# Splitting the mode mixing and the first GroupNorm into two halves of eight images

## The chip, the cores and the metric

The kernel runs on one core of one Trainium2 chip. The metric is the device time of one execution in microseconds (us), the median of three runs. Of one further execution there is a profile, taken by the hardware profiler.

## The reference

The input x has 16 images of 64 channels and 128 x 128 pixels, all in float32. Two layers are computed.

Layer 0: `x_ht = dht_2d(x)` (a Hartley transform); the lowest 20 x 20 modes are mixed over the channels, `0.5 * (e(x1, w1) - e(x1n, w1n) + e(x1, w1n) + e(x1n, w1))` with `e = einsum('bixy,ioxy->boxy')` and `n` for the mirrored mode; the result is transformed back, smoothed by a Gaussian along **all four** axes (images and channels too), and masked.

Layer 1, on that result: `h = group_norm(x)` in eight groups of channels; `afno(h)` (a Fourier transform, 32 x 32 modes, two complex block-diagonal layers with a Gelu between, the inverse transform) plus `h` plus `x`; a second group norm; `feats = gelu(conv1x1(h))`; two shared experts; a gating network on the mean of `feats` that picks 4 of 16 experts for each image; the sum of all of them plus the residual.

## The kernel before

The program is one long list of statements. A scheduler turns it into one queue for each engine and places every wait; a queue runs strictly in order.

**Forward (L239 to L266).** For each image b of 16, eight tiles `xt` (128 x 8 x 128, 512 KB) are loaded by SP (L245) into a pool of 10 buffers. TensorE multiplies each by `fwd1` (L250), ScalarE copies the product into `t1` (L253). After the second tile of the next image, `along_columns` takes the second axis: TensorE (L212), a ScalarE copy (L215), six VectorE additions (L219 to L222), and one VectorE operation for each of up to nine neighbouring images, which adds the Gaussian over images into `x2` (L231, L233). Image `bo` of `x2` is therefore final only when image `bo + 4` has passed. ScalarE then writes its mirrored second copy (L236, L237). Eleven pairs of loads bring the weights `wk` and `wn`.

**Mixing (L283 to L321).** For each of 11 values of k1, 20 matmuls with 64 weight columns and 64 moving columns (16 images, two copies, two modes; L294) fill one PSUM tile `psm`, which ScalarE and VectorE take turns to copy into `om` (L298 to L303). Then 128 small matmuls blur over channels (L312), and copies (L319, L321) make `ot`, 100 modes on the partitions.

**GroupNorm 1 (L397 to L471).** From `ot`: means (L397), deviations by a triangular matrix `dev` (L406), squared by ScalarE (L408), summed by `ones` (L412). The two halves of the images stand on the two halves of the partitions. A chain of small VectorE operations gives the scales `gs1`, and `st` for the modes.

**Fourier products (L539 to L565).** For each image and each half n of 1,024 modes: eight matmuls by the matrix `spec` (L548), VectorE scaling into `xk` (L552, L554), and, one step behind, the first complex layer (L499) with its Gelu (L501), stored to DRAM `o1d` (L503). `modes` (L480, L483) runs once for each of the first ten images, `modes_out` (L488 to L491) for the next four; it writes `od` and `ond` to DRAM, which the next stage reads back into `bm` (L611).

**Image stage (L571 to the end).** All the rest of layer 1, image by image, by a written-out order.

A matmul in float32 is recorded as two MATMUL and two LDWEIGHTS records, so a count of records is twice the count of matmuls. The profile numbers lines by this kernel:

Of the kernel before, what the change touches and what calls it, by code (L numbers as in the profile page):

```python
# [159 lines left out]
def hartley_afno_moe_kernel(ctx: ExitStack, tc: tile.TileContext, a: dict, out: bass.AP):  # L160
# [14 lines left out]
    on_modes = ExitStack()  # L175
    otp = on_modes.enter_context(tc.tile_pool(name="ot", bufs=1, side="right"))
    ot = otp.tile([CH, 4, NB * C], F32, name="ot")
# [9 lines left out]
    with tc.tile_pool(name="modes", bufs=1) as mp:  # L187

        x2 = mp.tile([P, 2, NB, NM], F32, name="x2")
        wk = mp.tile([P, K // 2 + 1, K, C], F32, name="wk")
        gb = blur_matrix(NB)
        with tc.tile_pool(name="f_x", bufs=10) as xp, tc.tile_pool(name="f_t", bufs=2) as tp, \
                tc.tile_pool(name="f_c", bufs=1) as fc, \
                tc.tile_pool(name="f_p1", bufs=4, space=PSUM) as pp1, \
                tc.tile_pool(name="f_p2", bufs=2, space=PSUM) as pp2:
            fwd1 = load(fc, "fwd1", [P, W1], nc.gpsimd)
            fwd2 = None

            wn = fc.tile([P, K, C], F32, name="wn")
            seen = set()

            def along_columns(b, t1):


                ps = pp2.tile([P, K // 2, W1], F32, name="ps2")
                for m in range(K // 2):
                    for t in range(2):
                        for h in range(2):  # L210
                            j = 2 * (2 * m + h) + t
                            nc.tensor.matmul(ps[h * C:(h + 1) * C, m, :], lhsT=t1[:, j, :],  # L212
                                             rhs=fwd2[:, j, :], start=(t == 0), stop=(t == 1))
                pn = tp.tile([P, K // 2, K], F32, name="pn")
                nc.scalar.copy(pn, ps[:, :, K:2 * K])  # L215
                xm = tp.tile([P, K, K], F32, name="xm")
                for half, op in ((0, ALU.add), (1, ALU.subtract)):
                    to = xm[half * C:(half + 1) * C]
                    nc.vector.tensor_tensor(to[:, 0:1], ps[0:C, 0:1, 0:K], pn[0:C, 0:1], op)  # L219
                    nc.vector.tensor_tensor(to[:, 2:K:2], ps[0:C, 1:, 0:K],  # L220
                                            pn[0:C, K // 2 - 1:0:-1], op)
                    nc.vector.tensor_tensor(to[:, 1:K:2], ps[C:P, :, 0:K],  # L222
                                            pn[C:P, ::-1], op)
                xf = xm.rearrange("p a b -> p (a b)")
                for bo in range(NB):
                    g = float(gb[bo, b])
                    if g == 0.0:
                        continue
                    to = x2[:, 0, bo, :]
                    if bo in seen:  # L230
                        nc.vector.scalar_tensor_tensor(to, xf, g, to, ALU.mult, ALU.add)  # L231
                    else:
                        nc.vector.tensor_scalar(to, xf, g, None, ALU.mult)  # L233
                        seen.add(bo)
                    if not gb[bo, b + 1:].any():
                        nc.scalar.mul(x2[0:C, 1, bo], x2[C:P, 0, bo], -1.0)  # L236
                        nc.scalar.copy(x2[C:P, 1, bo], x2[0:C, 0, bo])  # L237

            behind = None  # L239
            for b in range(NB):  # L240

                t1 = tp.tile([P, 2 * K, C], F32, name="t1")
                for c0 in range(0, C, 8):
                    xt = xp.tile([P, 8, N], F32, name="xt")
                    nc.sync.dma_start(xt, a["x"][b, :, c0:c0 + 8])  # L245
                    ps = pp1.tile([P, 8, W1], F32, name="ps1")
                    for i in range(8):
                        for h in range(2):
                            cols = slice(h * 64, (h + 1) * 64)
                            nc.tensor.matmul(ps[cols, i, :], lhsT=xt[:, i, cols],  # L250
                                             rhs=fwd1, start=True, stop=True)
                    src = ps[:, :, 0:2 * K].rearrange("p c j -> p j c")
                    nc.scalar.copy(t1[:, :, c0:c0 + 8], src)  # L253
                    if c0 == 8 and behind:
                        along_columns(*behind)
                behind = (b, t1)
                fwd2 = fwd2 or load(fc, "fwd2", [P, 2 * K, W1])

                if 0 < b <= K // 2 + 1:
                    k = b - 1  # L260
                    nc.scalar.copy(wk[C:P, k, 0], wn[C:P, 0])
                    nc.scalar.copy(wk[C:P, k, 1:K], wn[C:P, K - 1:0:-1])
                if b <= K // 2:
                    nc.sync.dma_start(wk[0:C, b], a["w"][b])
                    nc.sync.dma_start(wn[C:P], a["w"][(-b) % K])
            along_columns(*behind)  # L266

        sc = on_modes.enter_context(tc.tile_pool(name="s_c", bufs=1, side="right"))
        blurc = load(sc, "blurc", [P, C])
        dev = load(sc, "dev", [CH, 4, NM])  # L270
        mean = load(sc, "mean", [CH, 4, C])
        gn1 = load(sc, "gn1", [P, 2, C])
        ident = load(sc, "ident", [P, C])
        sel = load(sc, "sel", [CH, 5, 32])
        w1 = load(sc, "w1", [P, 2, P])
        vec = load(const, "vec", [P, V_N])
        spec = load(sc, "spec", [CH, 4, 2 * MD * MD])
        exw = load(sc, "exw", [P, C, NE])

        with tc.tile_pool(name="m_o", bufs=1) as op, \  # L280
                tc.tile_pool(name="m_p", bufs=2, space=PSUM) as pp, \
                tc.tile_pool(name="m_p2", bufs=4, space=PSUM) as pp2:


            om = [op.tile([P, NB, NM // 2], F32, name=f"om{h}") for h in range(2)]
            lok, upk = (t[h * C:(h + 1) * C].rearrange("o b (k2 k1) -> o k1 k2 b", k1=K)
                        for h, t in enumerate(om))
            for k1 in range(K // 2 + 1):

                ps = pp.tile([P, K // 2, 2, NB, 2], F32, name="psm")  # L290
                for m in range(K // 2):
                    k = k1 * K + 2 * m
                    for h in range(2):
                        nc.tensor.matmul(ps[h * C:(h + 1) * C, m].rearrange("p a b q -> p (a b q)"),  # L294
                                         lhsT=wk[:, k1, 2 * m + h, :], rhs=x2[:, :, :, k:k + 2],
                                         start=True, stop=True)
                lo, up = ps[0:C, :, :, :, 0], ps[C:P, :, :, :, 1]
                nc.scalar.copy(lok[:, k1], lo[:, :, 0])  # L298
                nc.vector.tensor_copy(upk[:, k1], up[:, :, 0])
                if k1 % (K // 2):  # L300
                    nc.scalar.copy(lok[:, K - k1, 0:1], lo[:, 0:1, 1])
                    nc.scalar.copy(lok[:, K - k1, K // 2 - 1:0:-1], lo[:, 1:, 1])
                    nc.vector.tensor_copy(upk[:, K - k1, ::-1], up[:, :, 1])  # L303


            for b0 in range(0, NB, 8):
                for cc in range(2):
                    pq = [pp2.tile([CH, 8, C], F32, name="pst") for h in range(2)]
                    for i in range(8):
                        for h, (m0, m1) in ((0, (0, C)), (1, (C, CH)), (1, (0, C)), (0, (C, CH))):  # L310
                            g = slice(h * C, (h + 1) * C)
                            nc.tensor.matmul(pq[h][m0:m1, i, :],  # L312
                                             lhsT=om[h][g, b0 + i, cc * CH + m0:cc * CH + m1],
                                             rhs=blurc[g], start=True, stop=True)
                    for h in range(2):
                        dst = ot[:, 2 * h + cc, b0 * C:(b0 + 8) * C]
                        src = pq[h].rearrange("p b c -> p (b c)")
                        if h:
                            nc.scalar.copy(dst, src)  # L319
                        else:  # L320
                            nc.vector.tensor_copy(dst, src)  # L321
# [49 lines left out]
    with tc.tile_pool(name="s_w", bufs=2) as sw, tc.tile_pool(name="s_o", bufs=1) as so, \  # L371
# [38 lines left out]
        for rc in range(4):  # L410
            for (g, cols), sq in zip(halves, sqs):
                nc.tensor.matmul(psv[g], lhsT=ones[:CH], rhs=sq[:, rc], start=(rc == 0), stop=(rc == 3))  # L412
# [547 lines left out]
```

## Time and profile before

| | |
|---|---|
| Three runs | 1852.95, 1852.01, 1849.28 us; median 1852.01 |
| Profiled execution | 1848.89 us, span 1846.9 us, mean granted clock 0.976 |
| TensorE, VectorE, ScalarE, GpSimd busy | 92 %, 69 %, 75 %, 7 % of the span |

By stage, from the view of busy time by windows of core 0 (us from the span's start):

| Stage | Window | Length | TensorE busy | Granted clock | DMA share |
|---|---|---|---|---|---|
| last part of the forward | 207.0 to 253.4 | 46.4 | 36.83 | 0.96 | 0.63 |
| TensorE waits for `x2` | 253.4 to 261.4 | 8.0 | 0 | 0.71 | 0.19 |
| channel products (L294) | 261.4 to 289.3 | 27.9 | 20.52 | 0.74 | 0.60 |
| blur over channels (L312) | 289.3 to 296.4 | 7.1 | 6.44 | 0.64 | 0.25 |
| GroupNorm 1 (L397, L406, L412) | 296.4 to 320.9 | 24.5 | 24.50 | 1.00 | 0.11 |
| Fourier products | 320.9 to 472.5 | 151.6 | 150.19 | 1.00 | 0.26 |
| image stage | 472.5 to 1846.9 | 1374.4 | 1314.43 | 0.99 | 0.26 |

How to read it: busy is the time in which at least one record of the engine ran; a DMA share of 1 means that all 16 DMA engines of the core were busy; the granted clock is what the throttle let TensorE have, 1 being full speed.

### The profile page before, as it was taken

What the parts mean: (1) busy time and instruction counts of PE and PEld (TensorE: products, weight loads), DVE (VectorE), ACT (ScalarE), POOL (GpSimd) and SP (SyncE); (2) the same over time, 40 slices, a digit from 0 to 9 for tenths busy, and PEclk for the clock granted to TensorE, in tenths of its full rate; (3) what the DMA queues carried; (4) which work ended last, traced back from release to release, by engine and by line L of the source; (5) the groups of instructions that cost most, each with busy time, mean ns of one, the idle gap of its engine ahead of it and who ended that gap; (6) DMA issues with size and microseconds to landing.
All of it is one profiled execution on the core that took longest, in us unless ns stands there. A gap on an engine that the chain in (4) does not pass through costs nothing. (4 is left out here: it accounts for less than half of the span.)

```text
span 1846.9 us, 55817 instructions
## 1 busy us (share of the span) xinstructions
PE 1701.5 (92%) x24644; PEld 940.8 (51%) x24644; DVE 1270.7 (69%) x1774; ACT 1378.3 (75%) x1690; POOL 120.9 (7%) x140
## 2 busy tenths in 40 slices
PE   6777769999899999999999999999999999999996
PEld 6776765333645455454545555454545455554521
DVE  1233432322249788797979797797979797887988
ACT  2343343112488998989898999989898999989897
POOL 0000002003010101010110101010100101010110
PEclk8899988999999999999999999999999999999998
DMA  9999841115212222222332222322232322222023
GB/s 337 319 322 326 285 145 48 69 52 145 47 25 70 48 81 57 84 36 82 57 72 58 59 82 36 99 41 81 37 86 53 71 72 46 72 57 71 27 72 92
DMA packets 136129, 181.00 MB, mean 98 GB/s; under 512 B 94201, under 2 KB 95414, under 8 KB 135658
## 3 DMA queue, kind: packets, MB, share of 16 engines
q1 hardware_dynamic: 132192, 171.73, 33.1%
q0 software_dynamic: 3696, 5.71, 1.2%
q8 instruction: 193, 3.16, 0.7%
q14 instruction: 48, 0.39, 0.1%
HBM read 98.29 MB, written 79.11 MB: 96 GB/s over the span
## 5 line engine op out<-in xcount | busy, mean ns | idle before, releaser
L834 DVE SCALAR_TENSOR_TENSOR h<-g,wt,h 128x1024 f32<-128x1024 f32 x512 | 620.9, 1275 | 85.2 <-ACT g L831 85.2
L831 ACT ACTIVATE g<-pe,wl 128x1024 f32<-128x1024 f32 x512 | 539.4, 1131 | 8.9 <-PE pe L826 8.2
L826 PE MATMUL pe<-f,wl 64*64 64x512 f32 x4096 | 494.7, 600 | 1.3 <-issue 0.4
L834 DVE SCALAR_TENSOR_TENSOR h<-g,h 128x1024 f32<-128x1024 f32 x256 | 301.6, 1220 | 56.1 <-ACT g L831 56.1
L831 ACT ACTIVATE g<-pe,vec_sb 128x1024 f32<-128x1024 f32 x256 | 278.7, 1135 | 20.6 <-PE pe L826 20.4
L669 PEld LDWEIGHTS pe<-inv_sb,u 107*128 107x128 f32 x2048 | 234.4, 192 | 64.9 <-ACT g L831 33.2
L826 PEld LDWEIGHTS pe<-f,wl 64*64 64x64 f32 x4096 | 135.6, 132 | 237.3 <-ACT g L831 98.6
L826 PE MATMUL pe<-f,shw 64*64 64x512 f32 x2048 | 252.9, 604 | 0.0
L669 PE MATMUL pe<-inv_sb,u 107*128 107x128 f32 x2048 | 248.8, 279 | 3.2 <-ACT g L831 1.9
L677 ACT ACTIVATE h<-pe,gs 128x1024 f32<-128x1024 f32 x128 | 142.6, 1115 | 73.2 <-PE pe L669 57.3
L250 PE MATMUL ps<-fwd_sb,xt 128*64 128x64 f32 x4096 | 141.5, 232 | 51.0 <-issue 43.1
L681 DVE BATCH_NORM_STATS2 stats<-h 128x6 f32<-128x512 f32 x256 | 160.1, 679 | 25.9 <-ACT h L677 25.8
L250 PEld LDWEIGHTS ps<-fwd_sb,xt 128*64 128x64 f32 x4096 | 135.9, 147 | 54.7 <-issue 46.6
L647 PE MATMUL pe<-inv_sb,bm 64*64 64x128 f32 (+1 forms) x4096 | 144.8, 275 | 1.2 <-issue 1.2
L736 ACT ACTIVATE f<-pe,fb 128x1024 f32<-128x1024 f32 x128 | 144.3, 1137 | 2.2 <-PE pe L732 2.2
L647 PEld LDWEIGHTS pe<-inv_sb,bm 64*64 64x64 f32 (+1 forms) x4096 | 118.5, 124 | 48.1 <-ACT f L736 24.3
L253 ACT COPY t<-ps 128x320 f32<-128x320 f32 x128 | 54.0, 427 | 114.4 <-PE ps L250 114.0
L732 PE MATMUL pe<-h,fs 64*64 64x512 f32 x1024 | 133.9, 611 | 1.6 <-DVE n L709 1.6
L652 ACT COPY u<-pe 105x1024 f32<-105x1024 f32 x128 | 127.4, 1043 | 3.9 <-PE pe L647 2.9
L219 DVE TENSOR_TENSOR xm<-ps,pn 64x20 f32<-64x20 f32 x32 | 5.5, 171 | 172.5 <-ACT pn L215 172.2
L548 PE MATMUL psx<-spec_sb,ot 100*64 100x512 f32 x512 | 115.6, 594 | 0.0
L806 POOL DMA_INDIRECT wl<-exd,ati x64 | 66.9, 1045 | 697.4 <-ACT g L831 605.4
(164 smaller groups left out, 1163.5 us busy)
## 6 DMA issues: line engine op xcount, KB each, us to landing
xt<-in_x_dram SPq DMA_DIRECT2D x128, 512.0 KB
out_dram<-h SPq DMA_DIRECT2D x256, 256.0 KB
o1d<-o SPq DMA_DIRECT2D x16, 512.0 KB
s<-o1d SPq DMA_DIRECT2D x16, 512.0 KB
bm<-od SPq DMA_DIRECT2D x96, 50.0 KB
wk<-in_w_dram SPq DMA_DIRECT2D x11, 320.0 KB
wn<-in_w_dram SPq DMA_DIRECT2D x11, 320.0 KB
spec_sb<-in_spec_dram SPq DMA_DIRECT2D x1, 3200.0 KB
```

What stands on the lines that cost most here:

```text
L250: nc.tensor.matmul(ps[cols, i, :], lhsT=xt[:, i, cols], rhs=fwd1, start=True, stop=True)
L548: nc.tensor.matmul(ps[ri * C:(ri + 1) * C], lhsT=ot[:, kc, b * C:(b + 1) * C], rhs=spec[:, kc, ri * 1024 + n * 512:ri * 1024 + (n + 1) * 512],
L647: nc.tensor.matmul(ps[cs, h, i, :], lhsT=bm[rs, 4 * q + i, cs], rhs=inv1[rs, part], start=True, stop=True)
L652: nc.scalar.copy(dst.rearrange("p h s n -> p n h s"), ps[0:KC].rearrange("p h s n -> p n h s"))
L669: nc.tensor.matmul(ps[:, r // 4, r % 4 * N:(r % 4 + 1) * N], lhsT=u[0:KU, 2 * row:2 * row + 2, :].rearrange("p h c -> p (h c)"), rhs=inv2, ...
L677: nc.scalar.activation(h, ps, AF.Identity, bias=gs1[:, 1, box["b"]:box["b"] + 1])
L681: nc.vector.bn_stats(box["stats"][:, 2 * t + p, :], h[:, p])
L732: nc.tensor.matmul(ps[p * C:(p + 1) * C, half], lhsT=box["fs"][rows_], rhs=box["h"][t][rows_, p], start=True, stop=True)
L736: nc.scalar.activation(f, ps, AF.Gelu, bias=box["fb"], accum_out=box["sums"][:, t:t + 1])
L826: nc.tensor.matmul(ps[half * C:(half + 1) * C, p], lhsT=w[rows_], rhs=f[rows_, half], start=True, stop=True)
L831: nc.scalar.activation(g, ps, AF.Gelu, bias=bias)
L834: nc.vector.scalar_tensor_tensor(h, g, share(), h, ALU.mult, ALU.add)
```

## The change

Mixing and GroupNorm 1 become a generator `behind_modes(h, ...)` that works on eight images (h = 0 or 1) and is advanced step by step among other work. Its first half is advanced once for each tile of the forward from image 12 on, when images 0 to 7 are final; its second half is advanced twice after each half of an image in the Fourier products of images 1 to 6. `x2` becomes `x3` with three blocks: the sums of images 0 to 7, one block of mirrored copies that both halves use in turn, and the sums of images 8 to 15. The constants are loaded after image 10's tiles and not after the forward; `spec` is loaded as eight tiles into the buffers of `xt`. Pools shrink: `xt` from 10 to 8 buffers, the forward's PSUM from 4 and 2 tiles to 3 and 1. `modes` and `modes_out` run after each half of images 8 to 14. The rest, the image stage included, is unchanged.

```diff
+    sc, sqp, xp = right("s_c", 1), right("s_q", 2), right("f_x", 8)
+    pm = on_modes.enter_context(tc.tile_pool(name="m_p", bufs=2, space=PSUM))
+    x3 = mp.tile([P, 3, HB, NM], F32, name="x3")
+    wn = om[1].rearrange("p b m -> p (b m)")[:, 0:K * C].rearrange("p (k c) -> p k c", c=C)
+    def second(bo):
+        sums = x3[:, bo // HB * 2, bo % HB]
+        nc.scalar.mul(x3[0:C, 1, bo % HB], sums[C:P], -1.0)
+        nc.vector.tensor_copy(x3[C:P, 1, bo % HB], sums[0:C])
...
+    def behind_modes(h, blurc, dev, mean, gn1, ident, sel, w1, vec):
+        if h:
+            for bo in range(HB, NB):
+                second(bo)
+                if bo % 2:
+                    yield
...
+        for k1 in range(K // 2 + 1):
+            ps = pm.tile([P, K // 2, 2, HB, 2], F32, name="psm")
+            for m in range(K // 2):
+                k = k1 * K + 2 * m
+                for i in range(2):
+                    nc.tensor.matmul(ps[i * C:(i + 1) * C, m].rearrange("p a b q -> p (a b q)"),
+                                     lhsT=wk[:, k1, 2 * m + i, :], rhs=x3[:, h:h + 2, :, k:k + 2],
+                                     start=True, stop=True)
...
+            yield
+        for cc in range(2):
+            pq = [pm.tile([CH, HB, C], F32, name="psm") for i in range(2)]
...
+            yield
...
+        psm = pm.tile([P, 512], F32, name="psm")
+        for kc in range(4):
+            nc.tensor.matmul(psm[g], lhsT=mean[:, kc, :], rhs=ot[h][:, kc], start=(kc == 0), stop=(kc == 3))
+        yield
...
+        for rc in range(5):
+            if rc < 4:
+                ps = pm.tile([P, 512], F32, name="psm")
+                for kc in range(rc, 4):
+                    nc.tensor.matmul(ps[:CH], lhsT=dev[:, kc, rc * CH:(rc + 1) * CH],
+                                     rhs=ot[h][:, kc], start=(kc == rc), stop=(kc == 3))
+                sq = sqp.tile([CH, 512], F32, name="sq")
+                nc.scalar.activation(sq, ps[:CH], AF.Square)
+                sqs.append(sq)
+            if rc:
+                nc.tensor.matmul(psv[g], lhsT=made["ones"][:CH], rhs=sqs[rc - 1], start=(rc == 1), stop=(rc == 4))
+            yield
...
+                if c0 == 8 and behind:
+                    along_columns(*behind)
+                if b == HB + 4 and c0 == 24:
+                    first = behind_modes(0, **consts)
+                elif first:
+                    next(first, None)
...
+            if b == K // 2:
+                consts = constants()
+        for n in range(2):
+            for kc in range(4):
+                t = xp.tile([P, 8, N], F32, name="xt")
+                spec[n, kc] = t[0:CH].rearrange("p a b -> p (a b)").rearrange("p (r j) -> p r j", r=2)
+                nc.sync.dma_start(spec[n, kc], src[:, kc, :, n])
+        along_columns(*behind)
+        for _ in first:
+            pass
...
+    last = behind_modes(1, **consts)
+    for b in range(HB - 1):
+        def between(n):
+            for _ in range(2 if b else 0):
+                next(last, None)
+        fourier(b, between)
+    for _ in last:
+        pass
+    mixing.close()
...
+        steps = [lambda m=m: modes(m) for m in range(K // 2)] + [lambda i=i: modes_out(i) for i in range(QB)]
+        for b in range(HB - 1, NB):
             if b == HB:
                 bn1s, bn1f, bn2s, bn2f = prepare()
+            def between(n):
+                if b >= HB and steps:
+                    steps.pop(0)()
+            fourier(b, between)
```

`fourier(b, between)` holds the Fourier products of one image as before and calls `between(n)` after each half. `consts` are the tiles that `constants()` loads.

## The prediction

> **What bounds the kernel now.** The chain of waits reaches back over the last few per cent only, so I read busy time by windows, cut where TensorE changes its work:
>
> ```profile
> core 0: us, PE busy (x) PEld busy (x) DVE busy (x) ACT busy (x) POOL busy (x), PEclk, DMA share, GB/s
> 207.00:253.40 46.40, 36.83 (x1153) 35.74 (x1149) 17.88 (x45) 15.95 (x39) 0.00 (x0) 0.96 0.63 221
> 253.40:261.40 8.00, 0.00 (x0) 0.00 (x0) 4.21 (x12) 5.59 (x11) 0.20 (x1) 0.71 0.19 55
> 261.40:289.30 27.90, 20.52 (x440) 19.42 (x440) 9.10 (x22) 9.84 (x35) 0.00 (x0) 0.74 0.60 161
> 289.30:296.40 7.10, 6.44 (x258) 6.24 (x258) 3.04 (x10) 4.37 (x16) 7.03 (x3) 0.64 0.25 67
> 296.40:320.90 24.50, 24.50 (x76) 9.02 (x74) 4.56 (x17) 6.65 (x10) 4.04 (x4) 1.00 0.11 18
> 320.90:472.50 151.60, 150.19 (x809) 49.28 (x806) 44.13 (x79) 28.12 (x39) 15.99 (x32) 1.00 0.26 84
> ```
>
> Image 7 of `x2` is final at 207, when image 11 has passed; the new schedule can differ in order from about there. The image stage begins at 472.5 and is the same in both kernels, so what counts is this stretch of 265.5 us. TensorE is busy for 24.50 of 24.50 us in GroupNorm 1 and for 150.19 of 151.60 in the Fourier products: work moved there costs its full length. Only three places have room: 9.6 us in the forward, 8.0 between forward and mixing, 8.0 in mixing and blur.
>
> What is the room in the forward? The answer for L250, what its engines waited for (TensorE and its weight loads together):
>
> ```profile
>   issue: 89.7, 47
>   ACT t L253: 1.3, 2
>   DMA xt<-in_x_dram: 1.1, 2
> ```
>
> Hardly any wait for x: 89.7 us go to "issue". Windows cut from gap to gap show what that is:
>
> ```profile
> 158.80:165.20 6.40, 3.89 (x126) 3.75 (x126) 1.82 (x5) 1.73 (x5) 0.00 (x0) 1.00 1.02 402
> 165.20:171.65 6.45, 4.17 (x127) 3.89 (x127) 1.74 (x7) 2.10 (x4) 0.00 (x0) 1.00 1.01 311
> 225.20:231.30 6.10, 3.89 (x127) 3.75 (x126) 1.74 (x7) 1.18 (x3) 0.00 (x0) 1.00 0.99 389
> 241.60:249.28 7.68, 7.62 (x253) 7.48 (x253) 4.48 (x12) 3.67 (x9) 0.00 (x0) 1.00 0.02 5
> ```
>
> A gap of about 2.2 us stands after every 126 or 127 matmul records, 253 with their weight loads; with DMA idle (0.02) two blocks pass without one. I read these as fetches of the next block of instructions, which queue behind the loads. Such a gap cannot be filled by other TensorE instructions: more records bring more gaps.
>
> **The change, part by part,** from 207.0 to the image stage.
>
> Constants (1.06 MB) now stand between the tiles of images 10 and 11. In SP's queue image 11's loads stand behind them. At the 319 to 337 GB/s of the forward they take 3.2 us. With DMA the late one they cost 3.2; with TensorE the late one (no wait for x) nothing. I take 1.6.
>
> The Trainium skill, "DMA: Bandwidth & Descriptors", section "Queues, rings and completion order", speaks against this edit: a transfer is spread over the largest number of engines up to 16 that divides its outer sizes, so 100 partitions get ten of sixteen. The row nearest is the stretch of mixing with `spec` loading, a DMA share of 0.60, which neither refutes nor settles it. By the page the constants would take an estimated 4.9 us and the sum would be up to 1.7 more.
>
> The forward's own records keep 46.4.
>
> Half h=0, the eight images on the forward's side. The channel products (L294 before, L266 in the changed kernel) have 440 records, as before, with 32 moving columns instead of 64. L294 ran at 33 ns a record at full clock (61 in 2.02 us, 270 to 273), L250, same weight width, at 32 (223 in 7.17). Two column groups run at once, so halving the columns gives 16 if the product sets the pace. Weight loads of 32, 64, 100 and 128 columns last 110, 138, 167 and 192 ns: 0.85 ns a column, 55 for 64, 27 with two at once; if they set the pace it stays at 27 to 32. I take 30: 13.2 us, bounds 7 and 14.
>
> The same skill, "TensorE: Matmul & The Clock Gate", section "Back-to-back issue gap", has a floor of about 25 ns between matmuls, an estimated 11.0 us and a sum 2.2 lower per half. Against that floor stands the Fourier inverse, with 32 weight columns in four groups:
>
> ```profile
> 472.60:473.60 1.00, 1.00 (x80) 1.00 (x81) 0.00 (x0) 0.00 (x0) 0.00 (x0) 1.00 0.35 147
> ```
>
> 80 records in 1.00 us, 13 ns each.
>
> Blur: half of 258 records in half of 6.44 busy us, 3.0 warm. GroupNorm: L406 took 17.48 us for 40 records of 512 columns, 0.437 each; 20 belong to each half of the images, so a half costs 8.6. Means (L397) and `ones` (L412) were 16 records each in 3.7 us, because the two image halves ran side by side on the two halves of the columns, 0.23 a record. Alone, a half's 8 records have nobody beside them: I take 0.43 each, 3.4 twice (lower end 1.85 each, should neighbours overlap as well). Half h=0: 13.2 + 3.0 + 8.6 + 3.4 + 3.4 = 31.6 us. Both halves are 63.2 where the old stages had 51.4 busy and 16.1 idle: doing it in halves eats most of the idle time it frees.
>
> Fetch: 604 more records in the forward are 4.8 blocks. The 9 blocks from 207 to 253 lost 9.6 us, 1.05 each: 5 us. Ends: 10 at 2 us each; and minus 7 if all 14 gaps shrink to 0.2, since x is then loaded more slowly than DMA could.
>
> Evacuation: a step of mixing took 2.5 us (27.9/11), because `psm` has two buffers and the chain ScalarE 0.45, VectorE 0.46, ScalarE 0.59, VectorE 0.45 empties them. Now a step stands behind each forward tile (32 records of L250 and 10 of L212 on average, 1.3 us), with VectorE (17.88 of 46.4) and ScalarE (15.95) less than half busy. What queues behind a waiting L266 is the next tile's L250, and behind that its L253. I take 3 us for 20 steps; ends 0 and 14 (eleven times 2.5 less 1.2).
>
> `spec` waits for `xt` buffers that image 15 frees. 1.6 MB of its second half are still due after the last tile, 5 us, covered by `along_columns` and the first half of image 0 (4.3 us): 2, ends 0 and 6.
>
> Half h=1, in the Fourier stage: 31.6, fetch 0.5 (DMA is at 0.26 there), and 2 us of waits: its steps are two in a row, and the second needs the first's `psm` emptied while image products, 4.3 us a half, follow: ends 0 and 8. ScalarE (28 of 151) and VectorE (44) have the room.
>
> Fourier products: unchanged, 151.6, less 2 where matmuls of one column group overlap neighbours. `modes_out` (products, VectorE, and its DMAs in GpSimd's queue, which holds nothing else then) now starts later, about 26 us before the end where it was 52; the last `bm` read landed about 30 us after `modes_out` began and is needed 6 us into the image stage. Slack about 2: nothing, end +5.
>
> The 8.0 us wait for mirrored copies and the clock of 0.50 behind it vanish, as images 0 to 7 are final long before; what is late next is TensorE itself.
>
> Sum: 1.6 + 46.4 + 31.6 + 5 + 3 + 2 + 34.1 + 149.6 = 273.3, against 265.5: 7.8 longer. The profiled execution, 1848.9 us, becomes 1856.7. The median is 3.1 above it (1852.0): 1859.8.
>
> **The rivals.** The measurement can tell about 0.2%, 3.7 us.
>
> A, the forecast: TensorE keeps its pace, the halves double the unpaired matmuls. 1855.8 to about 1866.
>
> B, faster: TensorE, with 32 us more to do, loads x more slowly, DMA leaves saturation and the fetch gaps fall to 0.2 (5 + 7 = 12 below the sum). For it: the row at 0.02. Against it: L294 waited 5.3 us for "issue" in three gaps, at a share of 0.60. From 4.1 us of it the kernel is no slower, from 11.5 clearly faster. The same would come of L266 at 16 ns, 12.4 below over both halves. One of them: about 1847.5; both: 1835.
>
> C, slower by more: the evacuation chain stays exposed in the forward (+11) or in Fourier (+6), or `od` to `bm` is exposed (+5): one gives 1865 to 1871, all three 1882.
>
> D, no change: half of B, 1848.3 to 1855.7.
>
> **How the numbers follow.** A 0.42, C 0.18, D 0.15, B 0.25. Predicted is A's 1860. For 8 in 10 the range takes all of A and D, most of C up to 1876, and of B the single effect with margin, down to 1842. Faster 0.25, same 0.15, slower 0.60.
>
> **What would show it.** In the profile after: the forward ends at about 295 instead of 253.4, the Fourier products at about 480 instead of 472.5. L266 at full clock has 30 ns a record; its idle goes to "issue", not to `om`. Unpaired 512-column records have 0.43 us each. The 0.50 clock is gone. I am wrong if the image stage starts at 472 or before; then either the gaps per 126 records have shrunk or L266 runs near 16 ns, and windows cut from gap to gap tell which. If L266 waits for `om` more than 8 us in all, C holds; if the image stage idles on `bm`, its second part.

## The result, and the profile after

Twelve runs of each kernel: 1852.62 us median after, 1852.76 before; ratio 0.9996, 95% interval 0.9984 to 1.0009. The change makes no difference that these runs can tell. The range (1842 to 1876) holds the time; the likeliest case, 1860 and slower, did not come. What came is case D, no change, which had a chance of 0.15. The profiled execution took 1849.19 us, span 1847.4.

Busy time by windows, cut where the forward and the Fourier products end. The columns are those of the rows shown in the prediction: length, TensorE's products and weight loads, VectorE, ScalarE, GpSimd, granted clock, DMA share, GB/s.

```profile
207.00:285.30 78.30, 72.19 (x1845) 59.56 (x1846) 36.45 (x100) 26.05 (x73) 0.00 (x0) 0.98 0.58 184
285.30:470.40 185.10, 183.41 (x1419) 74.94 (x1417) 63.06 (x135) 45.63 (x94) 27.06 (x39) 1.00 0.25 78
470.40:1847.40 1377.00, 1315.03 (x17696) 677.23 (x17696) 1125.83 (x1424) 1234.89 (x1392) 92.61 (x96) 0.99 0.26 63
```

The image stage starts at 470.4, not at the 480 of the forecast (472.5 before). The Fourier stage, with the second half in it, has 185.1 us, where the forecast gave 2 + 34.1 + 149.6 = 185.7. The forward is what came out otherwise: 78.3 us from 207, where 1.6 + 46.4 + 31.6 + 5 + 3 made 87.6. TensorE is idle in it for 6.1 us. The waits of that stretch say of what (us in total, times, longest):

```profile
PE psm L266 <- issue: 2.8, 3, 1.4
PE ps L410 <- issue: 2.4, 2, 2.0
PE ps L373 <- issue: 0.9, 2, 0.6
PE ps L373 <- ACT t L413: 0.5, 1, 0.5
```

The "issue" lines are the gaps that the prediction read as instruction fetches (the 2.0 us began 0.6 us ahead of this stretch); the last line is a wait for the copy into `t`. So about 5.6 of the 6.1 us are such gaps. No line names `om`, `spec` or x: the chain that empties `psm` costs TensorE nothing here.

That these gaps are fetches is supported by the profile's DMA queues. In the kernel before, the queue named "instruction" (q8) moved this (packets, MB, share of 16 engines), and two gaps of its forward end at 231.34 and 241.61 us:

```profile
q8 instruction: 193, 3.16, 0.7%
231.34 7.17 PE L250 MATMUL ps<-fwd_sb,xt 128*64 128x64 f32 x223 [2.24 <-issue]
241.61 0.74 PE L250 MATMUL ps<-fwd_sb,xt 128*64 128x64 f32 x17 [2.21 <-issue]
```

193 packets for 24,644 matmul records are one for every 128 records. One of them starts between 228.9 and 229.1 us and one between 239.2 and 239.4, and the two gaps begin at 229.10 and 239.40.

### The profile page after: what moved, and what is told of

Same layout as the page of the kernel before. It is cut to its first block, busy times and chain, and to the rows that moved or that the text cites. A ratio compares the mean times of both kernels' runs of the same rounds, so it can differ in the third digit from the quotient of the medians.

```text
span 1847.4 us, 56775 instructions
## 1 busy us (share of the span) xinstructions
PE 1718.2 (93%) x25084; PEld 953.7 (52%) x25084; DVE 1288.8 (70%) x1831; ACT 1373.0 (74%) x1706; POOL 120.6 (7%) x140
## 5 line engine op out<-in xcount | busy, mean ns | idle before, releaser
L889 ACT ACTIVATE g<-pe,vec_sb 128x1024 f32<-128x1024 f32 x256 | 276.8, 1135 | 15.4 <-PE pe L884 15.3
L410 PE MATMUL ps<-fwd_sb,xt 128*64 128x64 f32 x4096 | 147.7, 234 | 44.3 <-issue 34.7
L739 DVE BATCH_NORM_STATS2 stats<-h 128x6 f32<-128x512 f32 x256 | 159.9, 677 | 28.9 <-ACT h L735 28.9
L410 PEld LDWEIGHTS ps<-fwd_sb,xt 128*64 128x64 f32 x4096 | 140.6, 149 | 51.8 <-issue 43.5
L478 PE MATMUL psx<-xt,ot 100*64 100x512 f32 x512 | 123.3, 596 | 0.0
```

The costliest lines, as they stand in the source:

```text
L410: nc.tensor.matmul(ps[cols, i, :], lhsT=xt[:, i, cols], rhs=fwd1, start=True, stop=True)
L478: nc.tensor.matmul(ps[ri * C:(ri + 1) * C], lhsT=ot[b // HB][:, kc, b % HB * C:(b % HB + 1) * C], rhs=spec[n, kc][:, ri], start=(kc == 0), ...
L739: nc.vector.bn_stats(box["stats"][:, 2 * t + p, :], h[:, p])
L889: nc.scalar.activation(g, ps, AF.Gelu, bias=bias)
```

## Experiments

**Theories.** Theory 1: a fetch gap lasts as long as the DMA load of that moment makes it. With half h=0 among the tiles TensorE needs longer for a tile, x is loaded less densely, and the gaps, old and new, get shorter. That is the mechanism of rival B. Theory 2: the gaps follow the number of loads queued ahead, and two buffers fewer shortened them. Further questions were what the interleaving hides, what paces L266, and what constants and unpaired records cost.

**The kernel before, a second profile** (unchanged).

> The kernel before, unchanged, profiled a second time, to see how far its stage boundaries move between executions. If the stages of the first profile are typical: 207.0 us after 4231 TensorE records +- 20, forward end 253 +- 1, image stage start 472.5 +- 1, its length 1374 +- 1. If executions differ in the forward (fetch gaps against loads): 4090 to 4230 records at 207 and an image stage start of 471 to 477; then differences of 2 to 3 us between single profiles, this change's -2.1 among them, say nothing.

Measured: 1861.26 us.

```profile
207.00:263.40 56.40, 43.47 (x1366) 42.36 (x1365) 21.05 (x54) 18.54 (x43) 0.00 (x0) 0.97 0.66 234
263.40:271.70 8.30, 0.13 (x6) 0.03 (x2) 4.21 (x12) 5.67 (x12) 0.20 (x1) 0.65 0.18 48
271.70:483.90 212.20, 201.38 (x1572) 83.71 (x1572) 60.68 (x128) 48.80 (x99) 26.95 (x38) 0.95 0.29 86
```

The forward ends at 263.4, ten us later than in the first profile, with 1366 records left at 207 where that had 1153. Behind the forward both agree: 220.5 us to the image stage against 219.1, and an image stage of 1375.6 against 1374.4. So executions differ mostly in the forward, by more than the change moves, and a stage start of one profile compared with that of another tells nothing below some ten us. What can be compared are idle times, paces, and lengths of stages behind the forward.

**The changed kernel, a second profile** (unchanged).

> The changed kernel, unchanged, a second profile and its time on the same chip as the paired kernel. Ratio to before 0.999 to 1.001 as measured; image stage start 470.4 +- 1 if the first profile is typical, 468 to 474 if executions differ; its length 1377, or 1374 to 1382.

Measured: ratio to before 1.0016, interval 0.9998 to 1.0034; forward end 289.5, image stage start 473.8, its length 1380.2. The Fourier stage has 184.3 us (185.1 in the first profile). The two profiles of each kernel put the forward's end 22 to 36 us later than before (285.3 and 289.5 against 253.4 and 263.4); the forecast had 41. TensorE is idle for 8.0 us of the forward from 207 (6.1 in the first profile), 7.4 of them fetch gaps.

```profile
289.50:473.80 184.30, 183.44 (x1420) 70.24 (x1417) 63.07 (x135) 45.76 (x94) 27.20 (x39) 1.00 0.25 79
```

**Eight buffers in the kernel before.**

```diff
-tc.tile_pool(name="f_x", bufs=10) as xp
+tc.tile_pool(name="f_x", bufs=8) as xp
```

> The kernel before with 8 buffers for x instead of 10, nothing else. Theory 1 (how long a fetch gap lasts follows the DMA load of that moment): the load is as heavy as before (0.86 from 207 to 241), so the gaps stay at about 1.3 us per block of 126 records, TensorE is idle for about 8 us from 207 to 241, and the forward ends at 253 +- 1.5 us. Theory 2 (it follows the number of loads queued ahead, which two buffers fewer shorten): about 0.6 us a block, some 4 us idle, the forward ends at about 249. Time: 1849 +- 4 by the first, 1845 by the second.

**Half of the last loads left out**, in the kernel before and in the changed one.

```diff
-xt = xp.tile([P, 8, N], F32, name="xt")
-nc.sync.dma_start(xt, a["x"][b, :, c0:c0 + 8])
+if b < 12 or c0 % 16 == 0:
+    xt = xp.tile([P, 8, N], F32, name="xt")
+    nc.sync.dma_start(xt, a["x"][b, :, c0:c0 + 8])
```

> The kernel before, where the odd tiles of images 12 to 15 are not loaded; TensorE takes the tile before them again (leaves out half of the last four images). 8.4 MB less, 25 us of transfer. Theory 1 (load): share from 207 to 241 falls to 0.3 to 0.5, gaps to 0.2 to 0.5 us a block, the forward ends 4 to 7 us earlier, at 246 to 249, and the image stage starts at 466 to 469. Theory 2 (queue depth): ten loads are queued as before, gaps stay, end at 253. Theory 3 (the forward was bound by loads after all): the end comes about 12 us earlier.

> The changed kernel, where the odd tiles of images 12 to 15 are not loaded (leaves out half of the last four images). Theory 1 (a fetch gap lasts as long as the DMA load of that moment makes it): the share from 207 to 241 falls from 0.67 to 0.2 to 0.3, the gaps from 0.6 us a block to 0.1, TensorE is idle for 1 to 2 us from 207 to the forward's end instead of 6.1, which comes at 279 to 282. Rival (the gaps left are tied to the mixing steps): idle stays at 5 to 6 us, end at 285.

**More loads in the changed kernel.**

```diff
 nc.sync.dma_start(xt, a["x"][b, :, c0:c0 + 8])
+if b >= 12 and c0 % 16 == 0:
+    nc.sync.dma_start(more[b - 12, c0 // 16], a["x"][b, :, c0:c0 + 8])
```

> The changed kernel, with every second tile of images 12 to 15 also copied from DRAM to DRAM (16 copies of 512 KB, behind the tile's own load in SP's queue; nothing reads them). Theory 1 (load): the share from 207 to 285 rises from 0.58 to 0.85 or more, the gaps from 0.42 us a block to about 1.3, so idle TensorE rises from 6.1 to 14 to 19 us and the forward ends at 293 to 298, where the forecast had it (295). Theory 2 (queue depth): idle TensorE stays at 6 us, end at 285 to 287; any delay would be a wait for x.

Measured: 1853.95 us with eight buffers, 1846.22 and 1839.72 with fewer loads, 1862.49 with more, one run each. The windows from 207 to 241 us: first the two kernels as they are, before and changed, and then the four in this order:

```profile
207.00:241.00 34.00, 25.75 (x798) 25.07 (x794) 13.29 (x33) 11.65 (x28) 0.00 (x0) 0.95 0.86 299
207.00:241.00 34.00, 29.72 (x924) 29.07 (x925) 16.83 (x46) 12.11 (x44) 0.00 (x0) 0.95 0.67 214
```

```profile
207.00:241.00 34.00, 25.93 (x804) 25.34 (x800) 16.12 (x41) 12.15 (x28) 0.00 (x0) 0.95 0.80 279
```

```profile
207.00:241.00 34.00, 33.46 (x1115) 33.11 (x1113) 18.68 (x50) 15.42 (x37) 0.00 (x0) 0.99 0.27 83
```

```profile
207.00:241.00 34.00, 32.55 (x1118) 31.60 (x1116) 18.66 (x50) 14.34 (x49) 0.00 (x0) 1.00 0.38 113
```

```profile
207.00:241.00 34.00, 27.49 (x751) 26.98 (x751) 15.70 (x43) 9.41 (x32) 0.00 (x0) 0.85 0.83 307
```

The first number is the length, the second TensorE's busy time; the share stands before the last column. The same window of all kernels, those of the later experiments too, roughly sorted by share, with the idle time worked out for 126 records:

| Kernel | DMA share | TensorE idle, us | Records | Idle per 126 records |
|---|---|---|---|---|
| before, second profile | 0.87 | 10.5 | 759 | 1.74 |
| before | 0.86 | 8.25 | 798 | 1.30 |
| changed, more loads | 0.83 | 6.5 | 751 | 1.09 |
| before, eight buffers | 0.80 | 8.1 | 804 | 1.26 |
| changed, first half in one piece | 0.80 | 6.8 | 857 | 0.99 |
| changed, other operands | 0.77 | 5.4 | 858 | 0.79 |
| changed, with late constants; pairing; both; second half in one piece | 0.70, 0.71, 0.71, 0.65 | 2.6, 3.1, 4.4, 4.8 | 1012, 1008, 929, 971 | 0.33, 0.39, 0.60, 0.62 |
| changed, both profiles | 0.67, 0.71 | 4.3, 3.1 | 924, 1008 | 0.58, 0.39 |
| changed, fewer loads | 0.38 | 1.45 | 1118 | 0.16 |
| before, fewer loads | 0.27 | 0.5 | 1115 | 0.06 |

Theory 2 falls: two buffers fewer leave the gaps where they were. Half the loads take them away in either kernel, as theory 1 has it. With fewer loads the kernel before ends its forward at 247.4 us (246 to 249 expected) and begins its image stage at 464.3, earlier than the 466 to 469 expected. The changed kernel ends its forward at 279.1 (279 to 282 expected); it is idle for 2.4 us from 207, a little more than the 1 to 2 expected, but only 0.7 of that is gaps. With eight buffers the forward ended at 257.4, not at 253; that execution had 100 records fewer done by 207.

More loads show less than was expected. In the window the gaps grow, but 1.6 us of the idle time there are waits for the mirrored copies and for `om`. Over the whole forward, at a share of 0.73 in place of 0.58, TensorE is idle for 10.1 us, not 14 to 19:

```profile
PE psm L267 <- issue: 5.4, 3, 2.7
PE psm L267 <- DVE om L276: 1.6, 2, 1.2
PE psm L267 <- DVE x L214: 1.2, 1, 1.2
PE ps L413 <- issue: 1.0, 2, 0.6
```

Gaps are 6.4 us of it, no more than the 5.6 and 7.4 of the changed kernel. The forward ends at 295.7, inside the 293 to 298 expected, but for another reason in part: the clock was granted at 0.92 in place of 0.98, so its 1900 records took 41.4 ns each, not 39.1, another 4 us, and 48 more records were left at 207. So theory 1 is shown in one direction, by taking loads away; adding loads did not confirm it.

**The second half in one piece, ahead of the Fourier products.**

```diff
-last = behind_modes(1, **consts)
+for _ in behind_modes(1, **consts):
+    pass
...
-            for _ in range(2 if b else 0):
-                next(last, None)
+            pass
```

> The changed kernel, with the second half of mixing and GroupNorm 1 in one piece ahead of the Fourier products, not among them. By the forecast's numbers the half's TensorE work (31.6) stays, and what its place among the products hides comes out: about 8 us until images 8 to 15 have their mirrored copies, and the evacuation chain of 11 steps (2.5 less 1.2 each, 14 us): 15 to 22 us slower, ratio 1.008 to 1.012, with L266 waiting for om or for psm's buffers. Rival (the chain is shorter than a step of products with half the columns): only the 8 us, ratio 1.004.

Measured: ratio 1.0029, interval 1.0013 to 1.0045; image stage start 469.5. Neither theory: the stage from the forward's end has 186.3 us (185.1 and 184.3 in the changed kernel), of which TensorE is idle for 2.5. TensorE's timeline behind the forward (start, us, what, records) tells why:

```profile
283.16 6.17 PE L478 MATMUL psx<-xt,ot 100*64 100x512 f32 x26
289.65 3.69 PE L266 MATMUL psm<-x,wk 128*64 128x32 f32 x120 [0.32 <-DVE x L213]
293.14 1.09 PE L478 MATMUL psx<-xt,ot 100*64 100x512 f32 x4
294.03 2.50 PE L266 MATMUL psm<-x,wk 128*64 128x32 f32 x80
```

It is not one piece on the chip. The scheduler put products of image 0 ahead of the mixing and between its steps, and they cover the wait for the mirrored copies and the chain. What hides the second half is that two independent streams exist, not where the source advances the generator. The ratio is not told from the second measurement of the changed kernel (0.9998 to 1.0034), but lies above the first (0.9984 to 1.0009); the 0.8 to 1.2% of the forecast did not come in either case.

**The first half in one piece, behind the last tile.**

```diff
-                elif first:
-                    next(first, None)
```

> The changed kernel, with the first half in one piece behind the forward's last tile. TensorE work is the same. x loads are then dense again from 207 to 241, so by theory 1 (load) the fetch gaps come back as in the kernel before (8 us idle from 207 to 241 instead of 4), and the evacuation chain is exposed for 11 steps (up to 14 us): 10 to 18 us slower, ratio 1.005 to 1.010. Rival (interleaving in the forward hid nothing, the gaps do not depend on the load): ratio 1.000 to 1.002.

Measured: ratio 1.0106, interval 1.0074 to 1.0137, at the upper end of what theory 1 and an exposed chain gave together. TensorE is idle for 17.5 us from 207 to 281.8:

```profile
PE ps L410 <- issue: 11.1, 6, 2.8
PE psm L266 <- DVE om L271: 3.7, 1, 3.7
PE psm L284 <- ACT ot L287: 1.4, 1, 1.4
```

The gaps are back (11.8 us in all, 11.1 of them at L410; 5.6 and 7.4 in the changed kernel), with some 6 us of waits for the chain. So the loss is in part gaps and in part the chain. From 207 to the image stage this kernel needs 276.8 us, 13.4 more than the first profile of the changed kernel. The 6 us are also what the chain costs when no forward work stands beside it; the forecast's upper end was 14.

**Other operands for L266.**

```diff
-nc.tensor.matmul(ps[i * C:(i + 1) * C, m].rearrange("p a b q -> p (a b q)"),
-                 lhsT=wk[:, k1, 2 * m + i, :], rhs=x3[:, h:h + 2, :, k:k + 2],
+q4 = 2 * (m % 2) + i
+nc.tensor.matmul(psf[q4 * 32:(q4 + 1) * 32, m // 2 * C:(m // 2 + 1) * C],
+                 lhsT=x3[:, h + i, k1 % HB, 32 * m:32 * m + 32], rhs=wk[:, k1, 2 * m + i, :],
```

> The changed kernel, where the channel products take 32 columns of x as the stationary operand and the 64 columns of weights as the moving one, in four column groups of the array (leaves the right layout of the products out). Number of records the same. If loading the 64 weight columns sets L266's pace of 29 ns a record: 13 to 16 ns here, 6 us less in the forward and 6 us less in the Fourier stage, in all 12 us (ratio 0.9935). If the moving columns or the issue set it: 27 to 29 ns, no gain (ratio 1.000). If TensorE is not what bounds the forward behind 207: gain in the Fourier stage only, ratio 0.997.

Measured: ratio to before 1.0002, interval 0.9980 to 1.0024. The same place of the Fourier stage, in the changed kernel and then with other operands:

```profile
325.79 2.52 PE L266 MATMUL psm<-x,wk 128*64 128x32 f32 x80
328.10 3.68 PE L478 MATMUL psx<-xt,ot 100*64 100x512 f32 x16
```

```profile
326.65 1.32 PE L267 MATMUL psm<-wk,x 128*32 128x64 f32 x80
327.90 3.65 PE L479 MATMUL psx<-xt,ot 100*64 100x512 f32 x16
```

From start to next start, 80 records take 2.31 us (28.9 ns each) and 1.25 us (15.6 ns). Twice the moving columns come at half the time per record, so neither the moving columns nor the issue of a record set L266's pace. Loading 64 weight columns would explain it (the prediction's 27 ns, from 0.85 ns a column). But the edit also goes from two column groups to four, and the time per record in one group is much the same, 58 ns (2 x 28.9) and 62 ns (4 x 15.6): a fixed time for each record of a group would do as well. Against it stands the prediction's row of the Fourier inverse, where four groups had 80 records in 1.00 us: 50 ns for a record in one group, less than 58 and with twice the moving columns. So the weight load is the likelier cause; no run varied the weight columns alone. The Fourier stage is 178.9 us, 6.2 and 5.4 shorter than 185.1 and 184.3, as expected:

```profile
289.20:468.10 178.90, 178.05 (x1390) 62.92 (x1385) 62.43 (x135) 44.93 (x94) 27.12 (x39) 1.00 0.26 81
```

The ratio does not show it (0.997 was expected for a gain in that stage alone). The forward gives nothing: its end is at 289.2. There the share is 0.77 in place of 0.67, and idle time from 207 is 8.5 us at a granted clock of 0.94. By theory 1 that is what less work for TensorE brings where x can be loaded faster; some of the steps were also moved to other places (the first to 96.9 us), so it is not shown alone.

**The constants behind image 12's tiles.**

```diff
-if b == K // 2:
-    consts = constants()
+if b == K // 2 + 2:
+    consts.update(constants())
```

> The changed kernel, with the constants loaded behind image 12's tiles instead of image 10's. If loads are what paces the forward until image 7 is final (95 TensorE records fewer by 207 us in the changed kernel): the first step of mixing starts at 207 to 208 instead of 211, and the forward and everything behind it ends 3 us earlier, ratio 0.9985. The first use of a constant is at 241 us and SP reaches these loads at about 225, so no wait for them. Rival (TensorE paces the forward, the constants cost nothing): no change.

Measured: ratio 1.0023, interval 1.0004 to 1.0042; first L266 record at 210.2 us (211.1), 4136 TensorE records by 207, exactly as in the changed kernel. The expected gain (a first step at 207 to 208, ratio 0.9985) did not come: loading the constants between images 10 and 11 costs nothing that shows. That the changed kernel has fewer records by 207 than the 4231 of the kernel before lies within what executions differ by: the second profile of the kernel before has 4010.

**Means and sums of squares over both column groups.** Even and odd parts of the sums go to the two halves of the partitions; a ScalarE copy and a VectorE addition join them.

```diff
-nc.tensor.matmul(psm[g], lhsT=mean[:, kc, :], rhs=ot[h][:, kc], start=(kc == 0), stop=(kc == 3))
+nc.tensor.matmul(psm[halves[kc % 2]], lhsT=mean[:, kc, :], rhs=ot[h][:, kc], start=(kc < 2), stop=(kc >= 2))
...
+nc.scalar.copy(d, psm[halves[1 - h]])
+nc.vector.tensor_tensor(d, psm[g], d, ALU.add)
...
-if rc:
-    nc.tensor.matmul(psv[g], lhsT=made["ones"][:CH], rhs=sqs[rc - 1], start=(rc == 1), stop=(rc == 4))
+for q in {2: (0, 1), 4: (2, 3)}.get(rc, ()):
+    nc.tensor.matmul(psv[halves[q % 2]], lhsT=made["ones"][:CH], rhs=sqs[q], start=(q < 2), stop=(q >= 2))
```

> The kernel with late constants, and in addition means and sums of squares (L297, L319) split over both column groups of the array, even and odd parts, added by one ScalarE copy and one VectorE addition each. Unpaired records have 0.43 us each, paired 0.23: 16 records a half save 3.2 us, 6.4 in all, of which 1 to 2 come back where the sum waits. With 3 us of the late constants: 8 us less than the changed kernel, ratio 0.9957; rival (neighbouring records of the other column group overlapped with the unpaired ones already): as with late constants alone, 0.9985.

> The changed kernel with the paired means and sums of squares only. The kernel with late constants and pairing began its image stage at 465.3 where late constants alone gave 469.6: pairing is worth 4.3 us by these. If that holds: image stage start at 465 to 467, ratio to before 0.997 to 0.9985, to the changed kernel 0.9977. Rival (the 4.3 were a difference between executions): as the changed kernel, ratio 1.000.

Measured with late constants: ratio to before 0.9984, interval 0.9966 to 1.0003, beside 1.0023 for late constants alone. Pairing alone: median 1844.65 us, ratio 0.9970, interval 0.9947 to 0.9992, beside 1856.28 us and 1.0016 for the changed kernel on the same chip. Means of the second half, in the changed kernel and paired:

```profile
348.54 3.22 PE L297 MATMUL psm<-ot,mean_sb 100*64 100x512 f32 x7
351.17 0.64 PE L478 MATMUL psx<-xt,ot 100*64 100x512 f32 x1
351.60 0.59 PE L297 MATMUL psm<-ot,mean_sb 100*64 100x512 f32 x1
351.65 2.68 PE L478 MATMUL psx<-xt,ot 100*64 100x512 f32 x10
```

```profile
347.89 1.94 PE L297 MATMUL psm<-ot,mean_sb 100*64 100x512 f32 x8
349.61 2.80 PE L482 MATMUL psx<-xt,ot 100*64 100x512 f32 x12
```

Eight paired records take 1.72 us to the next start, eight unpaired ones 3.1 (348.54 to 351.65, one product of an image among them). The Fourier stage has 181.1 us, 3 to 4 less than 184.3 and 185.1:

```profile
284.90:466.00 181.10, 180.24 (x1444) 69.51 (x1444) 64.33 (x137) 46.85 (x96) 27.15 (x39) 1.00 0.25 79
```

The forward from 207 has 77.9 instead of 82.5 in the second profile of the changed kernel, which stands at nearly the same record at 207 (4020 and 4018). This version is faster than the kernel before, by 0.3%, and than the changed kernel by about 0.45% (1.0016 against 0.9970, whose intervals do not meet). With late constants in both, the difference is 0.4%.

## Why the prediction was right and wrong

**The account.** From 207.0 to the image stage the forecast had 273.3 us, and it was 263.4 in the first profile (266.8 in the second); before it was 265.5 (276.9).

| Term | Forecast | Measured |
|---|---|---|
| Forward's own records, busy | 36.8 of the 46.4 | 39.6: 1241 were left at 207 (1845 less 604), at the old 31.9 ns |
| Constants | 1.6 | none seen |
| Half h=0 on TensorE | 31.6 | 32.6 (72.19 less 39.6) |
| Idle in the forward, nearly all of it fetch gaps, old and new | 9.6 + 5 | 6.1 (8.0 in the second profile) |
| Evacuation chain, forward | 3 | 0 |
| `spec` | 2 | 0 |
| Half h=1 and Fourier products | 34.1 + 149.6 | 185.1 |

**The step that failed** is "Fetch": I took the 1.05 us a block of the old stretch for the new one, though its own sum made the stretch half as long again at the same number of loads. Both my rows, 2.2 us a block at a share of 1 and none at 0.02, stood in the prediction, and B named the mechanism; I gave it 0.25 and put A first, leaning on the mixing stage's 5.3 us at 0.60, of which the longest gap, 3.25 us, fell where `spec` was being loaded at a share of 0.68. The term measured 6.1 and 8.0 us, not 14.6. The missing 8.5 or 6.6 are over half of B's 12 us, and by themselves nearly turn the 7.8 longer of the forecast into no change. So the range held the time because it reached from A's side over half of B, not because the sum was right. A smaller failure is the chain: the copies have half the elements (0.30 us for L270, where L298 had 0.45), and work of the forward covers what is left.

**Right:** the 8 us wait for mirrored copies and the cold clock behind it are gone (0.98 and 1.00 granted), and the halves eat that gain: mixing and GroupNorm 1 had 67.5 us between the forward and the Fourier products (253.4 to 320.9), and now the halves add 32.6 to the forward and 33.5 to the Fourier stage (185.1 less 151.6). The pace of L266, 30 ns, was 28.9, and the lower end of 16 is what the other operands reach. Unpaired records at about 0.4 us were an avoidable term (3.1 us for eight, 1.7 paired), and pairing them gives a gain of 0.3% over the kernel before. Rival C did not come: no wait for `om` in the forward, and no wait for `bm` among those of the image stage's first 30 us.

**Rule and row.** In the Trainium skill, "TensorE: Matmul & The Clock Gate", "Back-to-back issue gap", gives a floor of about 25 ns between matmuls. The records of four column groups, at 15.6 ns each, go below it, and the measurement decides; a whole float32 matmul, two records, takes 31 ns. "DMA: Bandwidth & Descriptors" has ten of sixteen engines for 100 partitions, in the section "Why a DMA increments its semaphore by 16 and not by 1" (the prediction names another section). Ten of sixteen are 0.625. The stretch in which only `spec` was being loaded comes near it, with a flat share of 0.67 at 246 to 251 GB/s:

```profile
280.00:284.00 4.00, 3.25 (x103) 2.97 (x98) 1.49 (x4) 1.27 (x3) 0.00 (x0) 1.00 0.67 246
284.00:288.00 4.00, 4.00 (x65) 2.58 (x63) 1.97 (x7) 0.33 (x1) 0.00 (x0) 1.00 0.67 251
```

It costs nothing here, since TensorE did not wait for `spec`.

**Open:** what besides the share sets the length of a gap (with more loads a share of 0.73 over the forward brought no more gap time than 0.58); whether the weight load alone sets the pace of L266; why the forward of the same kernel ends at 253 in one execution and at 263 in another (its loads came at 320 and 306 GB/s until 207), and why the image stage, the same instructions in all of these kernels, has 1374 to 1382 us. Twelve runs of the changed kernel spanned 1847 to 1855 us on one chip and 1845 to 1860 on another.

## What to carry to other kernels

A gap for instructions is a price that depends on the DMA load beside it: work added to an engine in a stage full of loads thins out the loads, and may pay for part of itself by shorter gaps, so such gaps should be costed at the load that the changed kernel will have. Splitting work into halves to hide it costs whatever was paired across the halves; look for another way to pair it, here even and odd parts of one sum. And before judging a few us from two profiles, profile the same kernel twice.

## What the runs showed of the hardware

TensorE's idle time per 126 matmul records was 0.06 us at a DMA share of 0.27 and 1.3 and 1.74 at 0.86 and 0.87, with one packet on the instruction queue for every 128 records. With 128 rows, matmuls of 64 weight columns in two column groups ran at 28.9 ns a record with only 32 moving columns, those of 32 weight columns in four groups at 15.6 ns with 64: for these shapes it paid to have the wider operand on the moving side. The same kernel's forward ended at 253 and at 263 us in two executions.
